# fc1 by plain tiles in every image, taps paused behind the last products of k, and the next image's sums two products later

## The chip, the cores and the metric

The kernel runs on one core of a Trainium2 chip. The metric is the device time of one execution in microseconds (us), taken as the median of several runs. The engines are TensorE (PE in the profile, with its weight loads as PEld), VectorE (DVE), ScalarE (ACT), GpSimd (POOL) and SyncE (SP). POOL and SP mostly issue DMAs here.

## What is computed

Two layers over eight images of 384 channels and 32 x 32 points, all in float32. The first is a transformer block, the second a ConvNeXt block:

```python
# layer 0, xf: (8, 1024 tokens, 384)
xn = layernorm(xf, g1, beta1)
q, k, v = split(xn @ w_qkv.T + b_qkv)              # 8 heads of 48
attn = softmax(q @ k.T * SCALE)
x1 = (attn @ v) @ w_proj.T + b_proj + xf
xn2 = layernorm(x1, g2, beta2)
y = x1 + gelu(xn2 @ w_fc1.T + b_fc1) @ w_fc2.T + b_fc2     # hidden 1536
# layer 1, on y as (8, 384, 32, 32)
z = depthwise_conv_7x7(y) + dw_b
z = layernorm_over_channels(z)
z = gelu(z @ w1 + b1)                               # hidden 1536
gx = sqrt(sum over points of z * z)
nx = gx / (mean over channels of gx + 1e-6)
z = grn_gamma * (z * nx) + grn_beta + z
out = y + z @ w2 + b2
```

## The kernel before

**Stages.** The images b = 0 to 7 follow one another. In one image PE runs the q and k products, the products of v, the attention (scores L804 and products with v L824), the projection in two halves of 512 tokens (L746), fc1 in two halves (L405), fc2 (L486), and the two products of the ConvNeXt block of the image before (h, then o). The channels are 3 tiles of 128 partitions, the hidden layer is 12 tiles, and a plain product of one hidden tile with one half is three matmuls over the channels. A float32 matmul of 512 columns shows as two records.

**Products by thirds and by quarters.** Some products use a scheme with fewer multiplications: `tiles_by_thirds` (L448) makes a group of 3 x 3 x 2 blocks out of 15 products (of sums of weights and sums of inputs) instead of 18. The 15 stand in the order SINGLY = 6, 10, 3, 5, 12, 2, 0, 11, 1, 4, 14, 7, 9, 8, 13; a callback `behind(n)` runs after product n. DVE (L473, L476) and ACT (L478) combine the results. q and k use it in images 1 to 7 (two groups: i = 0 is q, i = 1 is k). Attention starts after product 9 of k's group; the products behind it are issued at step 2 of attention (`last_tile`). fc1 uses it in images 2 to 6 (`fast_fc1`, L217) for tiles 6 to 11 of the first half, over quarters of 256 columns (`gelu_group`), with sums of weights s_fc1 that image 0 makes, and sums of inputs that ten DVE operations make (L445).

**The convolution** of image b runs beside image b + 1's attention and MLP. DVE does most taps (L1225), in a chain. ACT does HELPED of the taps per channel tile as products in half tiles (L1260), and POOL adds each to the accumulator by an accumulating DMA (L1261). The tap's tile has four buffers, so the fifth tap waits until the first has landed.

**Order.** There is no free scheduler: `Flow` (L137) adds up nominal PE time as products are issued, and issues the next piece of each DVE or ACT chain when its time has come. A chain's `yield us` sets when its next piece follows. The list `hold` pauses DVE's convolution and the chains in `freely`; the list `quiet` pauses ACT's taps. `rest()` in `mlp` (L987) runs the second half of the projection, after which LN2 of that half is spawned (`layernorm`, L527: sums L508, subtraction L551, squares L562 and L565, scaling L582).

**Layernorms.** The sums over channels are matmuls with ones. LN3 of the convolved image b − 1 runs on both halves together (`abreast`; sums L522, the subtraction L551 reads them from PSUM). LN1 of image b + 1 (`norm_of_next`, L1936) has its own sums (L1961) and subtraction L1981. Both fall in the fc1 stage of image b. PSUM has two s tiles of two banks and four o tiles of one bank; the sums and fc1's tiles share them.

**The fc1 stage of images 2 to 6**, in order: group 0 of the quarters, tiles 0 and 1, rest(), tiles 2 to 5, group 1, then twelve tiles of the second half. In images 1 and 7: tiles 0 to 3, rest(), tiles 4 to 11, then the second half.

Of the kernel before, what the change touches and what calls it, by code (L numbers as in the profile page):

```python
# [52 lines left out]
B, C, H, W = 8, 384, 32, 32  # L53
N = H * W
CT = C // P
# [9 lines left out]
CM = 2  # L65
NC = HT // CM
U = 0.857
HELPED = 6, 7, 7
BEGUN = 5
SCALE = HD ** -0.5  # L70
EPS0, EPS1, GRN_EPS = 1e-5, 1e-6, 1e-6
# [105 lines left out]
def block_kernel(  # L177
# [28 lines left out]
    flow = Flow()  # L206
# [8 lines left out]
    s_fc1 = dram.tile([P, 2, len(FORMS), P], F32, tag="s_fc1", bufs=1, name="s_fc1")  # L215

    def fast_fc1(b):  # L217
        return not exact[0] and 1 < b < B - 1

    def half(h):  # L220
        return slice(h * NH, (h + 1) * NH)
# [302 lines left out]
            totals.append((total, cols))  # L524
        return totals

    def layernorm(src, dst, h, eps, g, name, switch, spare=None, spaced=False, slow=1.0, fold=None, wait=3.4, gentle=False, late=0, lag=0, fold_squares=True):  # L527

        cols = h if isinstance(h, slice) else half(h)
        if isinstance(h, slice):
            h = h.start
        width = cols.stop - cols.start
        if spare:
            a, *squares = (t[:, :width] for t in spare())
            rstd = a
        else:
            a = one.tile([P, NH], F32, tag="ln_a", name=f"{name}_a{h}")[:, :width]  # L540
        nc.vector.tensor_tensor(a, src[:, 0, cols], src[:, 1, cols], ALU.add)
        if gentle:
            yield 1.2
        nc.vector.tensor_tensor(a, a, src[:, 2, cols], ALU.add)
        yield 2.6 * max(slow, 1.0)
        totals = yield from token_sums(a, f"{name}_sum{h}", fold, wait)
        yield 0.8
        for ct in range(CT):
            for total, part in totals:
                to, of = dst[:, ct, cols][:, part], src[:, ct, cols][:, part]  # L550
                nc.vector.scalar_tensor_tensor(to, total, -1.0 / C, of, ALU.mult, ALU.add)  # L551
            if gentle:
                yield 1.2
        yield 0.8 * slow + lag
        if not spare:
            squares = [three.tile([P, NH], F32, tag="ln_sq", name=f"{name}_sq{h}_{ct}")[:, :width] for ct in range(CT)]
        for ct in range(CT):
            nc.scalar.activation(squares[ct], dst[:, ct, cols], AF.Square)
            if spaced:
                yield 1.7  # L560
        yield 0.8 if spaced else 1.8 * slow
        nc.vector.tensor_tensor(squares[0], squares[0], squares[1], ALU.add)  # L562
        if gentle:
            yield 1.2
        nc.vector.tensor_tensor(squares[0], squares[0], squares[2], ALU.add)  # L565
        yield 1.8 * slow
        if not fold_squares:
            fold = None
            yield wait
        totals = yield from token_sums(squares[0], f"{name}_var{h}", fold, wait)  # L570
        yield 0.8

        if not spare:
            rstd = one.tile([P, NH], F32, tag="ln_rstd", name=f"{name}_rstd{h}")[:, :width]
        if switch:
            ln_table()
        for var, part in totals:
            nc.scalar.activation(rstd[:, part], var, AF.Ln, bias=eps, scale=1.0 / C)
        nc.scalar.activation(rstd, rstd, AF.Exp, scale=-0.5)
        yield (2.6 if switch else 1.2) * slow + late  # L580
        for ct in range(CT):
            nc.vector.scalar_tensor_tensor(dst[:, ct, cols], dst[:, ct, cols], col(g, ct), rstd, ALU.mult, ALU.mult)  # L582
            if gentle and ct < CT - 1:
                yield 1.2

    def averages():
        return [attn[:, i, :] for i in range(4)]
# [48 lines left out]
    def qk(b, xn, weights=None):  # L636

        big = large_tile(b)  # L640
        wqk_sb = wqk_in(big)
        parts = big[:, : 2 * NP * N].rearrange("p (i m n) -> p i m n", i=2, m=NP)
        moves = [(own, other) for i in range(2) for own, other in pieces(lambda m: parts[:, i, m, :])]

        def finish(i, m, src, cols=slice(0, N)):
            at = i * CT + m
            bias = bqk[:, at : at + 1]
            nc.scalar.activation(parts[:, i, m, cols], src, AF.Identity, bias=bias, scale=1.0 if i else SCALE)  # L648

        def move(i, m):  # L650
            for own, other in moves[2 * (i * CT + m) : 2 * (i * CT + m) + 2]:
                nc.sync.dma_start(out=own, in_=other)

        def args(i, m):
            return lambda k: wqk_sb[:, k, i * CT + m, :], lambda k: xn[:, k, :], CT

        def finishing(i, m):
            yield 1.7
            finish(i, m, parts[:, i, m, :])
            move(i, m)  # L660

        chains = {}

        def ready(m):

            for key in list(chains):
                if m in (key[1], NP - 1):
                    flow.finish(chains.pop(key))

        def plain(i, m):  # L670
            finish(i, m, linear(*args(i, m), f"qk_{b}_{i * CT + m}"))
            move(i, m)

        def fast(i):
            tiles = {}

            def bank(name):
                name = "x" if name in "jqm" else name
                if name not in tiles:
                    tiles[name] = o_tile(f"qk_{b}_{i}_{name}")  # L680
                return tiles[name]

            c = {f"c{r + 1}{n + 1}": parts[:, i, CT - 1 - r, half(n)] for r in range(CT) for n in range(2)}

            def behind(n):
                if i and n == 7:
                    hold.append("k")
                if n in (4, 9, 13):
                    m = (4, 9, 13).index(n)
                    chains[i, m] = flow.spawn(finishing(i, m))  # L690

            return tiles_by_thirds(weights, f"qk_{b}", i, thirds["qk"], c, bank, behind)

        def last_tile():

            if weights:
                flow.finish(rest_of_k)
                return
            for h in range(2):
                finish(1, CT - 1, linear_half(*args(1, CT - 1), h, f"qk_{b}_last_{h}"), half(h))  # L700
            move(1, CT - 1)

        if weights:
            for _ in fast(0):
                pass
            rest_of_k = fast(1)
            for n in rest_of_k:
                if n == 9:
                    break
            return parts[:, 0], parts[:, 1], last_tile, ready  # L710

        for m in range(CT):
            for i in range(2):
                if (m, i) != (CT - 1, 1):
                    plain(i, m)
        return parts[:, 0], parts[:, 1], last_tile, ready
# [76 lines left out]
    def attention(b, xt, qT, kT, last_tile, ready, first, next_image):  # L793
# [44 lines left out]
        for n in range(len(steps) + 2):  # L838
            if n == 1:
                hold.clear()  # L840
            if n == 2:
                last_tile()
            if n < len(steps):
                if steps[n][0] == 0 and steps[n][2] == 0:
                    ready(steps[n][1])
                ps[n] = scores(*steps[n])
            if n >= 2:
                product(*steps[n - 2], ps.pop(n - 2))
            if n - 2 in (len(steps) // 2 - 9, len(steps) - 9):
                quiet.append("averages")  # L850
            if n - 2 == len(steps) // 2 + 6:
                for chain in first:
                    flow.finish(chain)
                xn = one.tile([P, CT, N], F32, tag="xn", bufs=2, name=f"xn2_{b}")
                for m in (NP - 1, *range(CT)):
                    flow.finish(chains[0, m])
                proj(b, xt, 0)
                quiet.clear()
                next_image(b)
                slow = {1: 1.35, B - 1: 1.2}.get(b, 1.0)  # L860
                fold = "columns" if b else None
                ln = layernorm(xt, xn, 0, eps0, "g2", f"ln2_{b}", False, spaced=True, slow=slow, fold=fold, wait=4.5)
                if fast_fc1(b):
                    ln = sequence(ln, make_quarters(xn, hidden(b), 1.5))
                ln = flow.spawn(ln)
# [121 lines left out]
    def mlp(b, xt, xn, weights, tag, ln, rest, before_fc2=None, behind_ln=None):  # L987
# [9 lines left out]
        for m in range(HT // 2 if fast else HT):  # L997
# [5 lines left out]
            if m == (1 if fast else 3) and rest:  # L1003
                rest()
                slow = 0.8 if fast else 1.2 if b == 1 else 1.0
                if fast:
                    hold.append("ln2")
                ln = flow.spawn(layernorm(xt, xn, 1, eps0, "g2", f"ln2_{b}", True, slow=slow))
                behind_ln(ln)
        if fast:  # L1010
            gelu_group(hid, 1, b, weights, waiting)
# [817 lines left out]
    def main():  # L1829
# [60 lines left out]
        def conv_norm(b, ln):  # L1890
# [5 lines left out]
            else:  # L1896
# [1 line left out]
                how = dict(wait=5.0, late=3.5 if b > 1 else 0, fold_squares=b > 1) if b < B - 1 else dict(factor=2.4, slow=1.5, lag=4.0)  # L1898
                norm = abreast(acc, acc, eps1, "lnw", f"ln3_{b - 1}", True, **how)
                if b < B - 1:  # L1900
                    state["norm1"] = flow.spawn(after(ln, freely(norm_of_next(b, 22.0 if b > 1 else 28.0))))
                    state["norm3"] = flow.spawn(after(ln, freely(sequence(end_soon(b), norm))))
                else:
                    state["norm3"] = flow.spawn(after(ln, after(state["help"], after(state["conv"], norm))))
# [31 lines left out]
        def norm_of_next(b, us):  # L1936
# [62 lines left out]
            for h, a, _ in pairs:  # L1999
                for ps, view in sums[h]:  # L2000
                    nc.scalar.activation(view(a), ps, AF.Ln, bias=eps0, scale=1.0 / C)
                nc.scalar.activation(a, a, AF.Exp, scale=-0.5)
            yield 45.0
            for h, a, _ in pairs:
                for ct in range(CT):
                    part = xn[:, ct, half(h)]
# [257 lines left out]
```

## Time and profile before

| what | us |
|---|---|
| median of three runs | 3239.14 (3237.69 to 3244.53) |
| profiled execution | 3245.64 |
| its span in the profile | 3243.9 |
| granted TensorE clock, mean | 0.997 |
| fc1 stage, images 3 and 4 (first product of fc1 to first of fc2) | 76.68, 75.53 |
| same, image 6 | 76.62 |
| ACT's waits for the DMA of a tap | 24.7, 21 times |

The profile is of a single execution. PE is busy nearly throughout, so the time is in the lengths of the stages on PE: a product that waits, or that runs at a lower granted clock, makes its stage longer. In the timeline a line is a run of like instructions: start, duration, engine, line, operation, tiles, shape, count, and in brackets the idle time before and what released it. [...]

### The profile page before, as it was taken

What the parts mean: (1) busy time and instruction counts of PE and PEld (TensorE: products, weight loads), DVE (VectorE), ACT (ScalarE), POOL (GpSimd) and SP (SyncE); (2) the same over time, 40 slices, a digit from 0 to 9 for tenths busy, and PEclk for the clock granted to TensorE, in tenths of its full rate; (3) what the DMA queues carried; (4) which work ended last, traced back from release to release, by engine and by line L of the source; (5) the groups of instructions that cost most, each with busy time, mean ns of one, the idle gap of its engine ahead of it and who ended that gap; (6) DMA issues with size and microseconds to landing.
All of it is one profiled execution on the core that took longest, in us unless ns stands there. A gap on an engine that the chain in (4) does not pass through costs nothing.

```text
span 3243.9 us, 39415 instructions
## 1 busy us (share of the span) xinstructions
PE 3213.5 (99%) x14204; PEld 1402.6 (43%) x14204; DVE 2540.3 (78%) x3578; ACT 1683.6 (52%) x2389; POOL 506.5 (16%) x607
## 2 busy tenths in 40 slices
PE   9999999999999999999999999999999999999999
PEld 5344434443444434444344443444435443344454
DVE  4548788897878978688777888778887788869964
ACT  3542763447644475453753637637375374742543
POOL 2102311012120121201212012120221202200000
PEclk9999999999999999999999999999999999999999
DMA  6525832557445564546636375363843638333244
GB/s 215 191 96 190 159 71 58 156 124 159 91 88 143 140 137 90 103 131 165 130 69 132 108 186 105 76 135 103 201 96 74 140 98 204 71 78 83 65 116 113
DMA packets 208741, 396.77 MB, mean 122 GB/s; under 512 B 42912, under 2 KB 49440, under 8 KB 208160
## 3 DMA queue, kind: packets, MB, share of 16 engines
q0 software_dynamic: 81984, 167.02, 27.2%
q1 hardware_dynamic: 126272, 226.49, 23.3%
q8 instruction: 114, 1.87, 0.2%
q10 hardware_dynamic: 288, 0.71, 0.1%
q14 instruction: 83, 0.68, 0.1%
HBM read 212.98 MB, written 40.11 MB: 78 GB/s over the span
## 4 chain that ended last, share of the span: by engine, by line
PE 86%; issue 5%; DMA 4%; DVE 3%; ACT 1%; POOL 1%; SPq 0%; POOLq 0%; DVEq 0%; ACTq 0%
PE fc L405 15%; PE s L804 13%; PE o L824 12%; PE fc_p L486 11%; PE o_p L486 6%; PE v L724 4%; PE proj L746 4%; PE h_n L457 3%; DMA acc<-tap 3%; PE h_z L457 3%; PE h_x L457 3%; PE h_last L1398 2%; PE o L1349 2%; PE h L392 2%; PE h_k L457 1%
## 5 line engine op out<-in xcount | busy, mean ns | idle before, releaser
L1225 DVE SCALAR_TENSOR_TENSOR acc<-pad,vec,acc 128x930 f32<-128x930 f32 (+8 forms) x808 | 905.5, 1157 | 5.7 <-DMA acc<-tap 2.5
L813 ACT ACTIVATE p<-s 128x1024 f32<-128x1024 f32 x512 | 523.9, 1025 | 250.3 <-PE s L804 242.3
L804 PE MATMUL s<-qk 48*64 48x512 f32 x4096 | 546.7, 592 | 10.0 <-ACT qk L648 8.6
L824 PE MATMUL o<-p,v 64*64 64x512 f32 x4096 | 541.8, 588 | 0.0
L405 PE MATMUL fc<-xn,fc 128*128 128x512 f32 x972 | 430.6, 599 | 0.0
L1261 POOL DMA_DIRECT2D acc<-tap x280 | 240.6, 873 | 1164.6 <-DVE gscale L1427 504.0
L486 PE MATMUL o_p<-y,w 128*128 128x512 f32 x664 | 289.0, 593 | 0.0
L804 PEld LDWEIGHTS s<-qk 48*64 48x64 f32 x4096 | 162.7, 133 | 289.1 <-issue 210.3
L405 PEld LDWEIGHTS fc<-xn,fc 128*128 128x128 f32 x972 | 185.5, 192 | 230.9 <-issue 224.6
L824 PEld LDWEIGHTS o<-p,v 64*64 64x64 f32 x4096 | 166.7, 132 | 274.3 <-issue 266.8
L486 PE MATMUL fc_p<-qk,fc 128*128 128x512 f32 x520 | 226.9, 593 | 0.0
L1260 ACT ACTIVATE tap<-pad,vec 128x512 f32<-128x512 f32 x280 | 206.3, 738 | 24.7 <-DMA acc<-tap 24.7
L486 PEld LDWEIGHTS o_p<-y,w 128*128 128x128 f32 x664 | 125.6, 190 | 157.7 <-issue 146.4
L1225 DVE SCALAR_TENSOR_TENSOR acc_last<-pad,vec,acc_last 128x377 f32<-128x377 f32 (+24 forms) x288 | 177.2, 688 | 0.6
L486 PEld LDWEIGHTS fc_p<-qk,fc 128*128 128x128 f32 x520 | 98.4, 190 | 123.6 <-issue 119.1
L498 ACT ACTIVATE qk<-fc,bfc_f 128x512 f32<-128x512 f32 x90 | 61.1, 684 | 141.9 <-PE fc L405 141.9
L498 ACT ACTIVATE hid<-fc,bfc_f 128x512 f32<-128x512 f32 x72 | 49.3, 687 | 159.1 <-PE fc L405 159.1
L765 DVE TENSOR_TENSOR attn<-o,attn 128x512 f32<-128x512 f32 x64 | 44.1, 689 | 110.9 <-ACT attn L763 109.2
L746 PE MATMUL proj<-attn,wproj_sb 128*128 128x512 f32 x288 | 127.3, 595 | 1.1 <-ACT b_f L1706 0.6
L974 ACT COPY pad<-x 128x512 f32<-128x512 f32 x42 | 26.4, 635 | 196.1 <-DVE x L1064 196.1
L724 PE MATMUL v<-wv_sb,xn 128*128 128x384 f32 x384 | 126.8, 487 | 0.0
L724 PEld LDWEIGHTS v<-wv_sb,xn 128*128 128x128 f32 x384 | 72.5, 190 | 50.1 <-issue 3.3
(445 smaller groups left out, 4610.3 us busy)
## 6 DMA issues: line engine op xcount, KB each, us to landing
acc<-tap POOLq DMA_DIRECT2D x280, 256.0 KB, 3.7
fc<-s_fc SPq DMA_DIRECT2D x91, 256.0 KB, 4.5
w<-s_w SPq DMA_DIRECT2D x91, 256.0 KB, 2.7
w<-s_w SPq DMA_DIRECT2D x72, 320.0 KB, 4.2
fc<-in_wfc SPq DMA_DIRECT2D x54, 384.0 KB, 4.2
y<-y POOLq DMA_DIRECT2D x38, 512.0 KB, 6.8
qk<-qk POOLq DMA_DIRECT2D x30, 512.0 KB, 7.4
qk<-s_qk SPq DMA_DIRECT2D x42, 320.0 KB, 5.1
```

The costliest lines, as they stand in the source:

```text
L405: nc.tensor.matmul(out=ps, lhsT=lhsT(k), rhs=rhs(k)[:, half(h)], start=(k == 0), stop=(k == nk - 1))
L457: nc.tensor.matmul(out=at, lhsT=weights.at(wname, g, slot // 5)[:, slot % 5, :], rhs=rhs[n], start=first, stop=True, skip_group_check=not ...
L486: nc.tensor.matmul(out=bank, lhsT=lhsT, rhs=rhs, start=k == 0, stop=k == len(pairs) - 1)
L498: nc.scalar.activation(dst, src, function, **kw)
L724: nc.tensor.matmul(out=ps[:, :C], lhsT=xn[:, k, t * P : (t + 1) * P], rhs=wv_sb[:, k, :], start=(k == 0), stop=(k == CT - 1),)
L746: nc.tensor.matmul(out=ps, lhsT=wproj_sb[:, m, ct * P : (ct + 1) * P], rhs=attn[:, m, :], start=(m == 0), stop=(m == CT - 1),)
L804: nc.tensor.matmul(out=s[64 * i : 64 * i + 64, j, :], lhsT=kT[64 * j : 64 * j + HD, m, k0 : k0 + 64], rhs=qT[64 * j : 64 * j + HD, m, half ...
L813: nc.scalar.activation(p, s, AF.Exp)
L824: nc.tensor.matmul(out=outs[i][64 * j : 64 * j + 64, :], lhsT=v[keys, t, at : at + 64], rhs=p[keys, j, :], start=(t == 0), stop=(t == KT - 1),
L1225: nc.vector.scalar_tensor_tensor(dst, window, tap, dst, ALU.mult, ALU.add)
L1260: nc.scalar.mul(t.rearrange("p (h w) -> p h w", w=W), window, tap)
L1261: nc.gpsimd.dma_start(out=acc[:, ct, half(h)], in_=t, accum_op=ALU.add)
```

## The change

It has four parts.

1. `fast_fc1` is False for every image: the quarters are gone, with their DVE sums of inputs and their loads of weight sums; images 2 to 6 use the order of images 1 and 7. The pauses "group" and "ln2" go with it. The new argument `apart` of `layernorm` is never other than 0, since `fast` is False. s_fc1 is still made in image 0, and read by nothing.
2. In k's group, `quiet` gets "k" after product 2 (the sixth in order) and `hold` gets "k" after product 0 (the seventh). Before, only `hold` did, after product 7 (the twelfth). Both are cleared at step 1 of attention.
3. The delay before LN1's sums in images 2 to 6 is 25.0 for 22.0, and a later delay in the same chain is 42.0 for 45.0.
4. HELPED is 5, 7, 7 for 6, 7, 7: one tap of the first channel tile goes from ACT to DVE.

The lines of the changed kernel stand two lower from L686 on, three lower from L840 on (L746 becomes L748, L1961 becomes L1964).

```diff
-HELPED = 6, 7, 7
+HELPED = 5, 7, 7
...
     def fast_fc1(b):
-        return not exact[0] and 1 < b < B - 1
+        return False
...
-    def layernorm(src, dst, h, eps, g, name, switch, spare=None, spaced=False, slow=1.0, fold=None, wait=3.4, gentle=False, late=0, lag=0, fold_squares=True):
+    def layernorm(src, dst, h, eps, g, name, switch, spare=None, spaced=False, slow=1.0, fold=None, wait=3.4, gentle=False, late=0, lag=0, fold_squares=True, apart=0):
...
-            if gentle and ct < CT - 1:
-                yield 1.2
+            if (gentle or apart) and ct < CT - 1:
+                yield apart or 1.2
...
             def behind(n):
-                if i and n == 7:
+                if i and n == 2:
+                    quiet.append("k")
+                if i and n == 0:
                     hold.append("k")
...
             if n == 1:
                 hold.clear()
+                quiet.clear()
...
-                ln = flow.spawn(layernorm(xt, xn, 1, eps0, "g2", f"ln2_{b}", True, slow=slow))
+                ln = flow.spawn(layernorm(xt, xn, 1, eps0, "g2", f"ln2_{b}", True, slow=slow, apart=1.3 if fast else 0))
...
-                    state["norm1"] = flow.spawn(after(ln, freely(norm_of_next(b, 22.0 if b > 1 else 28.0))))
+                    state["norm1"] = flow.spawn(after(ln, freely(norm_of_next(b, 25.0 if b > 1 else 28.0))))
...
-            yield 45.0
+            yield 42.0
```

## The prediction

> **What bounds the kernel now.** I read four views in this order: the head of the page, the chain of waits, the table of windows over the fc1 stages, and the waits of PE with the timeline around the two longest.
>
> ```profile
> span 3243.9 us, 39415 instructions
> ...
> PE 3213.5 (99%) x14204; PEld 1402.6 (43%) x14204; DVE 2540.3 (78%) x3578; ACT 1683.6 (52%) x2389; POOL 506.5 (16%) x607
> ...
> PE 86%; issue 5%; DMA 4%; DVE 3%; ACT 1%; POOL 1%; SPq 0%; POOLq 0%; DVEq 0%; ACTq 0%
> ```
>
> PE sets the end. It never rests for long, so time can only be won by fewer products, or by products that run at full pace. At full pace a product (two records of 512 columns) takes 0.858 us (records follow each other every 0.429 us in the timeline). "Busy 99%" hides slow products: a matmul that waits or runs at a lower clock counts as busy. So I compare lengths of like stages, from the fc1 stage's first product to fc2's first (the columns are busy time of PE, weight loads, DVE, ACT and POOL, then the clock, the DMA share and GB/s):
>
> ```profile
> 479.31:552.84 73.53, 73.53 (x184) 31.91 (x183) 60.03 (x77) 27.10 (x38) 8.97 (x10) 1.00 0.23 46
> 873.50:950.12 76.62, 74.66 (x208) 37.04 (x207) 53.67 (x88) 33.37 (x54) 9.76 (x11) 0.98 0.32 70
> ...
> 2065.11:2140.47 75.36, 73.27 (x210) 36.37 (x207) 52.78 (x86) 32.58 (x52) 9.32 (x11) 1.00 0.32 71
> ```
>
> The first row is image 1, which already runs fc1 by plain tiles: 73.53 us. Images 2 to 6 run the quarters: 76.62, 76.68, 75.53, 75.36, 76.62, together 380.81. The form with fewer multiplications is the longer one. Where it goes:
>
> ```profile
> PE s L804 <- ACT qk L648: 8.6, 7, 2.4
> PE fc_n L457 <- DVE qk L473: 8.0, 5, 1.6
> PE ln_sum L1961 <- PE ln_sum L1961: 1.7, 5, 0.4
> ...
> ACT tap L1260 <- DMA acc<-tap: 24.7, 21, 3.2
> ```
>
> The second line is the quarters' own wait, 1.6 us in each of five images. The first is the start of attention behind the k tiles; the last is ACT held by a tap's buffer. The third looks like nothing, yet what follows it in image 3 is dear:
>
> ```profile
> 1337.60 1.08 PE L522 MATMUL ln_sum<-attn,ones 64*64 64x512 f32 x4
> 1338.61 0.71 PE L1961 MATMUL ln_sum<-ln,ones 32*128 32x256 f32 x6
> 1339.65 0.67 PE L1961 MATMUL ln_sum<-ln,ones 32*128 32x256 f32 x2 [0.34 <-PE ln_sum L1961]
> 1340.25 8.83 PE L405 MATMUL fc<-xn,fc 128*128 128x512 f32 x16
> ```
>
> Its windows:
>
> ```profile
> 1336.50:1340.20 3.70, 3.36 (x17) 1.02 (x16) 2.53 (x5) 0.00 (x0) 0.00 (x0) 1.00 0.19 63
> 1340.20:1344.20 4.00, 4.00 (x7) 1.65 (x7) 4.00 (x9) 1.70 (x3) 0.00 (x0) 0.57 0.00 0
> ```
>
> 3.7 us of partial-array sums, then 4.0 us at a granted clock of 0.57: sixteen records took 8.83 us, where 16 × 0.429 = 6.9.
>
> **What the Trainium skill says.** "TensorE: Matmul & The Clock Gate", Part 1 (The HAM clock gate): the clock is half or full, decided by activity over windows of about 3.4 us. The trace agrees (0.57 over the 4.0 us after the sums; 1.00 in images 4 and 5 at the same place, so whether a window is caught depends on phase). The same page, "Architectural detail", says ACT and DVE run strictly in order. The trace agrees: L648 stands behind a tap that waits up to 3.2 us for a DMA. "Trainium Kernel Development and Optimization", Key Constraints: all queues' DMAs share the same 16 engines. The trace agrees where taps land late: the DMA share is 0.85 at the k boundary of image 7.
>
> **The change part by part.**
>
> *1. Quarters to plain tiles, five images.* A quarter group's start-to-next-start is 6.83 us (7.16 in image 5) for group 0 and 8.45 for group 1 with its 1.6 us wait, 15.3 together; 18 plain products are 18 × 0.858 = 15.44. Cost: +0.16 × 5 = +0.8 us, the lost multiplications paid by the lost wait. Ten DVE operations per image (L445, 413 ns) and three chunk loads on SP's queue go too; neither was on PE's path. With the loads gone the residual rows of the projection (r, L785) are no longer queued behind weights on SP.
>
> *2. Projection and LN2.* rest() moves from after tile 1 to after tile 3: the second projection half starts 12 products, about 10.3 us, into the stage instead of 12.0–12.3, and needs its last operand about 1.7 us later, at 12.0. That operand (L791, 685 ns) ended 11.1–13.4 us in, in images 2–6, at 10.14 in image 1. I bound the wait by 0 (image 1) and 1.4 us (13.4 − 12.0), and take 0.3 per image, 1.5 in all, because the loads that delayed r are gone. LN2 loses its hold, so DVE's taps (1.157 us) stand between its operations. Image 1 runs so already: its last L582 ended at 516.6, the second half began about 519.6, 3 us to spare.
>
> *3. Sums.* The next image's first sums (L1961, then L1964) now stand two products behind LN3's (L522), then one product follows. The eight-bank PSUM is what still binds: fc1's next bank waits for three L551 (3 × 0.611), the sums' bank for the other three. From the order in which instructions stand, two products (1.7 us) plus the sums (1.0) reach the bank 0.3–0.4 us too early, twice. Estimated loss 1.5 us per image with L522's own cost, 7.5 in all. Before, L522, L1961 and the slow products cost 4.30, 4.34, 3.09, 2.67, 4.30 = 18.7 over their full-pace time, image 1 0.94. Gain 18.7 − 7.5 = 11.2. The yield of 42 for 45 keeps the end of norm_of_next where it was.
>
> Parts 1–3 check against the stage lengths: 380.8 − 5 × 73.53 = 13.2 if the five stages were as short as image 1's; less 5 × 0.55 for the sums left together, less 1.5 for the projection: 8.9. The terms give 11.2 − 0.8 − 1.5 = 8.9.
>
> *4. The k boundary.* Before, only the convolution was held, from the twelfth of 15 products; now ACT's taps pause from the sixth and DVE's from the seventh, until the second step of attention. 28 products are 24.02 us; the seven q/k stages (images 1–7) took 24.13, 24.74, 26.60, 25.45, 25.50, 25.07, 26.63: 9.96 over. In image 3 the cause is plain:
>
> ```profile
> 1147.85 0.74 ACT L1260 ACTIVATE tap<-pad,vec 128x512 f32<-128x512 f32 x1 [2.53 <-DMA acc<-tap]
> 1148.49 1.13 ACT L648 ACTIVATE qk<-qk,bqk 128x1024 f32<-128x1024 f32 x1
> ```
>
> PE at the same place, and in image 7, with a window of image 7:
>
> ```profile
> 1149.68 1.95 PE L804 MATMUL s<-qk 48*64 48x512 f32 x16 [1.96 <-ACT qk L648]
> ...
> 2736.84 3.69 PE L804 MATMUL s<-qk 48*64 48x512 f32 x16 [2.43 <-ACT qk L648]
> ...
> 2733.00:2745.00 12.00, 9.57 (x36) 2.83 (x38) 6.95 (x10) 7.41 (x8) 4.22 (x5) 0.72 0.85 176
> ```
>
> Image 7 also restarts slowly: sixteen scores in 3.69 us instead of 1.95, and its attention is 124.54 us where others have 122.1–122.5. With no tap ahead of the last L648, I leave 0.15 per image: gain 9.0, plus about 2.0 in image 7's attention: 11.
>
> Queued behind the pause: some ten ACT taps with their POOL accumulations, and DVE's chain. Neither is due until LN3, in the fc1 stage. There the burst of ten taps that ended the convolution at about 38.6 us falls away; in the new order the last DVE tap stands at 35.2 and the last ACT tap at 24.0.
>
> *5. HELPED 6 to 5.* One tap per image from ACT to DVE, 7 × 1.157 = 8.1 us on an engine 78% busy; hidden beside PE, cost 0; if the convolution's end came to bind, up to 8.1.
>
> *6. fc2.* LN3's six L582 (742 ns) now stand before the differences that fc2 needs. In the new order these (L1067) come about 0.7 us ahead of need; range 0 to 0.7 × 5 = 3.5 us lost. I take 0, since the 8.9 above already carries a cautious projection.
>
> **Sum.** 8.9 + 11 = 20 us. The profiled execution took 3245.64 (span 3243.9 and 1.7 around it) and would become 3225.7. The median is 6.5 us lower, so I carry the same saving over: 3239.1 − 20 = 3219.
>
> **The rivals.**
>
> *A, forecast (0.60):* both stalls go, residuals as above. 3219, own range 3213 to 3226.
>
> *B, half of it (0.15):* the stall moves. The bank waits still trip the clock in three images (about 1.7 us more each, 5.1), the differences for fc2 come 0.7 late in five (3.5), k keeps a third of its loss (3.3): gain 8, 3231. For it: one tap still stands ahead of the last L648.
>
> *C, more (0.10):* no clock dips and no residuals: 13.2 + 12.5 with the other attentions' slight losses (images 3, 4 and 6, 0.5 us each): about 3213.
>
> *D, a trade (0.08):* the slow window comes wherever sums stand, so step 3's 11.2 are gone, and the paused taps crowd into the first steps of attention and give back 7 of the 11 at k: 20 − 11.2 − 7 leaves 2, so 3237. Against: image 1 shows sums that stand apart, without a dip.
>
> *E, slower (0.07):* LN2 without its hold. Six dependent DVE steps each wait behind one tap of 1.157 us, 6.9 us, plus the projection's 1.4; less image 1's 3 us of slack, 5.3 us of idle PE before the second half, in five images, and an idle of that length brings a slow-clock window, about 1.7 us more: 7.0 × 5 = 35. Then 3239 − 20 + 35 = 3254. It decides from 4 us per image on (20 / 5). For it: DVE's instructions in the new order, times their durations, make about 32 us of work for the 35 us concerned. Against: image 1.
>
> **How the numbers follow.** The measurement can tell about 0.2%, 6.5 us. A, most of B and C are faster by more: 0.84. D with B's tail is within: 0.09. E: 0.07. Range 3210 to 3235: it holds A and C nearly whole and B; left out are E and most of D.
>
> **What would show it.** fc1 stages of images 2–6 near 74.5 us; no L457 wait on L473; L1964 no longer beside L522, clock 1.00 in the eight us behind L522; no L1260 between the last k product and L648, the wait of scores on L648 under 2 us in sum; q/k stages at 24.1–24.3. Against me: a wait of the projection on L793 over 1 us, a wait on xn (L582) at the second half, a wait of fc2 on L1067, or a granted clock under 0.9 behind L522.

## The result, and the profile after

The changed kernel took 3224.26 us (median of six runs, 3223.74 to 3229.43); the kernel before, run again beside it, 3244.51 (3237.69 to 3249.71). The ratio is 0.9945, 95% interval 0.993 to 0.9959: faster by 13 to 23 us. The profiled execution went from a span of 3243.9 us to 3222.6, 21.3 us less. The prediction was 20 us less, and 3219.

The head of the page and the waits of PE, after:

```profile
span 3222.6 us, 38795 instructions
...
PE 3207.6 (100%) x14084; PEld 1376.6 (43%) x14084; DVE 2490.1 (77%) x3425; ACT 1662.6 (52%) x2325; POOL 494.7 (15%) x593
...
PE 93%; issue 2%; DMA 2%; DVE 1%; POOL 1%; ACT 0%; SPq 0%; POOLq 0%; DVEq 0%; ACTq 0%
```

```profile
PE h_n L457 <- DVE y L473: 2.9, 6, 0.5
...
PE h_k L457 <- DVE y L476: 1.0, 5, 0.2
...
PE s L806 <- ACT qk L648: 0.2, 1, 0.2
PE proj L748 <- DVE attn L793: 0.2, 1, 0.2
```

The scores' wait on L648 went from 8.6 us to 0.2, and the quarters' wait on L473 is gone. On top stands a wait that was not there before: the h products (the first product of the ConvNeXt block) wait for DVE's combinations.

PE is busy in both kernels, so the account is again one of stage lengths, from one stage's first product on PE to the next one's. The sums are over the images named. Of the rest, image 0's attention is 0.3 us shorter, image 7 from fc1 to the end of the kernel 0.4 longer, and the other stages changed by 0.1 us or less.

| stage (us) | before | after | gain | predicted |
|---|---|---|---|---|
| q/k, images 1 to 7 | 178.12 | 168.91 | 9.2 | 9.0 |
| attention, images 1 to 7 | 858.03 | 851.57 | 6.5 | 2.0 |
| fc1 with the second projection half, images 2 to 6 | 380.80 | 369.55 | 11.3 | 8.9 |
| fc2, images 1 to 6 | 321.86 | 321.86 | 0.0 | 0 |
| h, images 1 to 6 | 312.99 | 318.24 | −5.3 | 0 |

Two of the windows over fc1, after (the first is image 1, the second image 3), with the columns as before:

```profile
479.10:552.76 73.66, 73.66 (x184) 31.92 (x183) 63.44 (x80) 27.26 (x38) 8.87 (x10) 1.00 0.23 46
...
1265.84:1339.72 73.88, 73.76 (x186) 32.04 (x183) 49.22 (x71) 33.46 (x48) 13.25 (x16) 1.00 0.30 57
```

And the k boundary of image 3 after, ACT and then PE:

```profile
1141.24 0.59 ACT L478 COPY qk<-qk_x 128x512 f32<-128x512 f32 x1 [0.27 <-PE qk_x L457]
1142.89 1.15 ACT L648 ACTIVATE qk<-qk,bqk 128x1024 f32<-128x1024 f32 x1 [1.07 <-DVE qk L473]
```

```profile
1143.61 1.02 PE L457 MATMUL qk_n<-thirds,qk 128*128 128x512 f32 x2
1144.56 1.95 PE L806 MATMUL s<-qk 48*64 48x512 f32 x16
```

No tap stands between the copy and L648 now. L648 waits for its operand only, and the scores follow k's last product without an idle bracket.

### The profile page after: what moved, and what is told of

Its sections match the earlier page's. It is cut to its first block, busy times and chain, and to the rows that moved or that the text cites. A ratio compares the mean times of both kernels' runs of the same rounds, so it can differ in the third digit from the quotient of the medians.

```text
span 3222.6 us, 38795 instructions
## 1 busy us (share of the span) xinstructions
PE 3207.6 (100%) x14084; PEld 1376.6 (43%) x14084; DVE 2490.1 (77%) x3425; ACT 1662.6 (52%) x2325; POOL 494.7 (15%) x593
## 4 chain that ended last, share of the span: by engine, by line
PE 93%; issue 2%; DMA 2%; DVE 1%; POOL 1%; ACT 0%; SPq 0%; POOLq 0%; DVEq 0%; ACTq 0%
PE fc L405 17%; PE s L806 12%; PE o L826 12%; PE fc_p L486 11%; PE o_p L486 11%; PE proj L748 4%; PE v L726 3%; PE h_n L457 3%; PE h_z L457 2%; PE h_x L457 2%; PE h_last L1401 2%; PE o L1352 2%; PE h L392 2%; PE qk_n L457 2%; PE qk_z L457 2%
## 5 line engine op out<-in xcount | busy, mean ns | idle before, releaser
L1228 DVE SCALAR_TENSOR_TENSOR acc<-pad,vec,acc 128x870 f32<-128x870 f32 (+8 forms) x815 | 909.5, 1157 | 2.5
L806 PE MATMUL s<-qk 48*64 48x512 f32 x4096 | 539.3, 590 | 0.2 <-ACT qk L648 0.2
L405 PE MATMUL fc<-xn,fc 128*128 128x512 f32 x1152 | 505.5, 594 | 0.6
L1264 POOL DMA_DIRECT2D acc<-tap x266 | 227.4, 861 | 1357.6 <-ACT tap L1263 642.9
L405 PEld LDWEIGHTS fc<-xn,fc 128*128 128x128 f32 x1152 | 216.6, 190 | 280.6 <-issue 261.4
L486 PE MATMUL fc_p<-hid,fc 128*128 128x512 f32 x728 | 319.0, 594 | 0.0
L498 ACT ACTIVATE hid<-fc,bfc_f 128x512 f32<-128x512 f32 x192 | 131.6, 686 | 343.7 <-PE fc L405 343.6
L486 PEld LDWEIGHTS fc_p<-hid,fc 128*128 128x128 f32 x728 | 137.4, 190 | 174.9 <-issue 169.3
L1263 ACT ACTIVATE tap<-pad,vec 128x512 f32<-128x512 f32 x266 | 195.1, 736 | 5.3 <-DMA acc<-tap 5.3
L748 PE MATMUL proj<-attn,wproj_sb 128*128 128x512 f32 x288 | 127.4, 596 | 0.8 <-ACT b_f L1709 0.6
L551 DVE SCALAR_TENSOR_TENSOR acc<-ln_sum,acc 128x512 f32<-128x512 f32 x42 | 25.7, 681 | 93.6 <-PE ln_sum L522 93.6
```

The source lines that it names most:

```text
L405: nc.tensor.matmul(out=ps, lhsT=lhsT(k), rhs=rhs(k)[:, half(h)], start=(k == 0), stop=(k == nk - 1))
L486: nc.tensor.matmul(out=bank, lhsT=lhsT, rhs=rhs, start=k == 0, stop=k == len(pairs) - 1)
L498: nc.scalar.activation(dst, src, function, **kw)
L748: nc.tensor.matmul(out=ps, lhsT=wproj_sb[:, m, ct * P : (ct + 1) * P], rhs=attn[:, m, :], start=(m == 0), stop=(m == CT - 1),)
L806: nc.tensor.matmul(out=s[64 * i : 64 * i + 64, j, :], lhsT=kT[64 * j : 64 * j + HD, m, k0 : k0 + 64], rhs=qT[64 * j : 64 * j + HD, m, half ...
L1228: nc.vector.scalar_tensor_tensor(dst, window, tap, dst, ALU.mult, ALU.add)
```

## The experiments

Every time is compared with runs of the kernel before on the same chip, so the ratios can be set side by side; the changed kernel's is 0.9945. The four below ran first.

**k_only: the pause alone.**

```diff
 # in the kernel before
-                if i and n == 7:
+                if i and n == 2:
+                    quiet.append("k")
+                if i and n == 0:
                     hold.append("k")
...
             if n == 1:
                 hold.clear()
+                quiet.clear()
```

> The kernel before with the pause of the taps behind k alone (ACT's taps from the sixth of k's products, DVE's from the seventh, both until step 1 of attention). Theory: the last bias addition of k (L648) no longer stands behind a tap that waits for a DMA; the seven q/k stages take 24.1 us each (9 us in sum), and the attentions of images 2 to 7 lose their slow starts (5 to 6 us): 14 to 15 us faster than before, about 3229; the fc1 stages stay at 75.4 to 76.7. Rival (the paused taps crowd into attention and fc1 and take it back): the q/k stages shorten, but attention or fc1 grow, and no more than 7 us are left.

3230.55 us, ratio 0.9965 (0.9953 to 0.9977), 11 us faster. In its profile all seven q/k stages are 24.13 us, and the attentions of images 1 to 7 add up to 851.69, as after. These two give 15.5 us, of which 11.1 are left in the span, because this execution's attention of image 0 took 137.26 us instead of 133.41 (last section). The fc1 stages stayed long. The theory holds for the stages; the median is 3 us short of the lower end of what I expected, though 14 us lies within the interval. A pause moves taps, and nothing of the q/k gain came back elsewhere.

**no_k: the changed kernel without the pause.**

```diff
 # in the changed kernel
-                if i and n == 2:
-                    quiet.append("k")
-                if i and n == 0:
+                if i and n == 7:
                     hold.append("k")
...
-                quiet.clear()
```

> The changed kernel with the old pause behind k (the convolution alone, from the twelfth product). Theory: the q/k stages are back at 24.7 to 26.6 us and attention at 122.5: 14 to 15 us slower than the changed kernel, about 3239. Rival (plain fc1 and the tap moved from ACT had a share in it): less than 8 us slower.

3241.06 us, ratio 0.9993 (0.9984 to 1.0001): about 15.6 us above the changed kernel by the ratios. q/k stages 24.13 to 26.03. Without the pause, the other three parts together can hardly be told from no change. In its profile they do show: the fc1 stages are 10.9 us shorter in sum, the h stages 5.3 longer. The gains of k_only and no_k add up to 13.6 us where the changed kernel has 17.8 by its ratio; the intervals are wide enough for that.

**plain_only: plain fc1 alone** (the quarters' two pauses go with it).

```diff
 # in the kernel before
     def fast_fc1(b):
-        return not exact[0] and 1 < b < B - 1
+        return False
```

> The kernel before with fc1 by plain tiles in all images, and nothing else. Theory (the sums that stand together are what made the fc1 stage long, not the quarters): LN1's sums still follow LN3's at once, so the fc1 stages of images 2 to 6 stay at about 76 us, within 1 us of before, and the h stages grow by 1 us each because LN1's scaling comes earlier: 2 to 6 us slower than before. Rival (the quarters' wait on DVE and their loads were the cost): fc1 stages of about 74 us, 6 to 11 us faster than before.

3240.36 us, ratio 1.0 (0.9991 to 1.0008). Neither came true as a whole. The fc1 stages fell to 74.75 to 74.79, 373.8 in sum: 7.0 us less than before. The h stages of images 2 to 6 grew by 0.68 each, 3.4 in sum. The sums in image 3, and windows from them on:

```profile
1327.63 0.65 PE L522 MATMUL ln_sum<-ln_a,ones 64*64 64x512 f32 x2
1327.64 0.65 PE L522 MATMUL ln_sum<-attn,ones 64*64 64x512 f32 x2
1328.11 0.60 PE L522 MATMUL ln_sum<-ln_a,ones 64*64 64x512 f32 x2
1328.12 0.59 PE L522 MATMUL ln_sum<-attn,ones 64*64 64x512 f32 x2
1328.65 0.71 PE L1961 MATMUL ln_sum<-ln,ones 32*128 32x256 f32 x8
1330.78 4.53 PE L405 MATMUL fc<-xn,fc 128*128 128x512 f32 x10 [1.42 <-DVE acc L551]
```

```profile
1327.60:1330.80 3.20, 1.78 (x18) 0.57 (x17) 2.05 (x4) 0.69 (x1) 0.69 (x1) 1.00 0.68 118
1330.80:1334.80 4.00, 4.00 (x10) 1.85 (x11) 4.00 (x8) 1.72 (x4) 0.00 (x0) 1.00 0.27 45
```

Two things differ from before. LN3's two groups of sums start together (1327.63 and 1327.64) where they ran one after the other (1336.54 and 1337.60), and the clock behind them is full. The bank wait is not gone, it is 1.42 us in one piece. A slow window behind the sums cost 1.55, 1.81 and 1.62 us in images 2, 3 and 6 before, 5.0 of the 7.0.

**old_sums: the changed kernel with the old delays.**

```diff
 # in the changed kernel
-norm_of_next(b, 25.0 if b > 1 else 28.0)
+norm_of_next(b, 22.0 if b > 1 else 28.0)
...
-            yield 42.0
+            yield 45.0
```

> The changed kernel with the old delays of LN1's chain (22 and 45), so that LN1's sums follow LN3's at once. Theory: the fc1 stages of images 2 to 6 are back at about 76 us, with a granted clock below 0.9 behind the sums in some of them: 9 to 12 us slower than the changed kernel, about 3234. Rival (the plain order alone mends it): within 2 us of the changed kernel, fc1 stages at 74 us.

3229.98 us, ratio 0.9964 (0.995 to 0.9978), about 6 us above the changed kernel; its profile has one of the long attentions of image 0 (137.28). The fc1 stages are 74.70 each, 4.0 in sum over the changed kernel's, with the same wait of 1.4 us for L551 behind L1964 as in plain_only and no slow window. So most of what I had put down to the two products' distance comes with the plain order already.

The next four went together.

**late_scale: where LN1's scaling falls.**

```diff
 # in the changed kernel
-            yield 42.0
+            yield 51.0
```

> The changed kernel with one number altered: the later delay in LN1's chain is 51 where it is 42, so that LN1's scaling (L2010) stands 13.8 us into the h stage instead of 5.2 (before: 12.0). Theory (the h stages of images 2 to 6 grew from 52.17 to 53.15 us because DVE does LN1's scalings there just where a group's first results must be combined): the h stages are back at 52.2, about 5 us faster than the changed kernel, near 3219. Rival (the tap that went from ACT to DVE did it): the h stages stay at 53.15 and the time stays.

3224.38 us, ratio 0.9944 (0.9933 to 0.9956). The h stages are 52.95, not 52.2: neither side. In the trace the first scaling starts 14.7 us into the stage, and PE's wait for L473 has moved on by one product, from h_n to h_z (2.6 us in six waits).

**helped6: the moved tap put back.**

```diff
 # in the changed kernel
-HELPED = 5, 7, 7
+HELPED = 6, 7, 7
```

> The changed kernel with HELPED back at 6, 7, 7. Theory (the moved tap lies beside PE's work wherever it is): within 2 us of the changed kernel, the h stages still 53.15. Rival (the tap on DVE crowds the h stage): the h stages go to 52.2 and the kernel is 5 us faster.

3225.82 us, ratio 0.9945 (0.9933 to 0.9957), h stages 53.15. The tap is hidden in either place, and is not what lengthens the h stages.

**act_pause and dve_pause: one engine's taps paused, not both.**

```diff
 # act_pause, in the changed kernel
-                if i and n == 0:
+                if i and n == 7:
                     hold.append("k")
 # dve_pause, in the changed kernel
-                if i and n == 2:
-                    quiet.append("k")
```

> The changed kernel with ACT's taps paused from the sixth of k's products as it has it, but DVE's convolution held only from the twelfth, as before. Theory (an ACT tap that waits for its buffer ahead of L648 was the whole cause): q/k stages of 24.1 us, within 2 us of the changed kernel. Rival (DVE's taps delay the combination that L648 reads): q/k stages of 24.5 to 25, 3 to 6 us slower than the changed kernel.

> The changed kernel with DVE's convolution held from the seventh of k's products as it has it, but no pause of ACT's taps. Theory: q/k stages of 24.7 to 26.6 us, 12 to 16 us slower than the changed kernel, as with the old pause. Rival: q/k stages near 24.5, less than 6 us slower.

act_pause: 3226.1 us, ratio 0.9946 (0.9934 to 0.9957), q/k stages 24.13 in all images. dve_pause: 3238.76, ratio 0.9987 (0.998 to 0.9993), q/k stages up to 26.64. ACT's pause is the whole of the k gain, as far as the intervals tell. ACT at the boundary of image 3 in dve_pause:

```profile
1146.05 0.59 ACT L478 COPY qk<-qk_x 128x512 f32<-128x512 f32 x1
1148.02 0.74 ACT L1261 ACTIVATE tap<-pad,vec 128x512 f32<-128x512 f32 x1 [1.38 <-DMA acc<-tap]
1148.66 1.13 ACT L648 ACTIVATE qk<-qk,bqk 128x1024 f32<-128x1024 f32 x1
```

The tap is back ahead of L648, with its DMA wait, though DVE's chain was held. That the wait counts, and not the tap, is seen in the kernel before: in images 2 to 7 the tap ahead of the last L648 had waited 1.5 to 3.2 us, and the stages are 0.6 to 2.5 us longer than 24.13; in image 1 two taps stand there that waited for nothing, and the stage is 24.13.

**scale49, sums28_45, sums18_56: the h stages and the sums again.** By the nominal PE time that orders the instructions, all three put LN1's scaling 12.0 us into the h stage, where the kernel before had it, and the changed kernel 5.2; in the trace its first operation then starts 14.1 us into the stage before and in scale49, and 5.4 after. The last two move the sums as well.

```diff
 # scale49, in the changed kernel
-            yield 42.0
+            yield 49.0
 # sums28_45: 28.0 and 45.0 for 25.0 and 42.0
 # sums18_56: 18.0 and 56.0 for 25.0 and 42.0
```

> The changed kernel with the later delay of LN1's chain at 49, where it is 42: LN1's scaling stands 12.0 us into the h stage, just where the kernel before had it (51 put it at 13.8, 42 at 5.2). Theory (what counts is where in a group of h products DVE's scaling falls, and before it fell where no combination was due): the h stages of images 2 to 6 are back at 52.2 us, about 5 us off the profiled span, near 3219 in the median. Rival (something else of the plain order sits in the h stage): 52.9 or more, as with 51.

3221.8 us, ratio 0.9935 (0.9919 to 0.9951); the span is 2.7 us shorter. The h stages of images 2 to 6 are 52.18, 52.18, 52.17, 52.17 and 52.43; that of image 1 grew from 52.51 to 53.61, since the same number moves its scaling too. Together 3.5 us less. In the h stage of image 3 of the changed kernel PE waits twice, 0.21 and 0.55 us. DVE's first scaling there, and what stands on DVE and PE at the second wait:

```profile
1398.64 0.74 DVE L2010 SCALAR_TENSOR_TENSOR xn<-xn,vec,ln 128x512 f32<-128x512 f32 x1
...
1410.30 1.09 DVE L1244 SCALAR_TENSOR_TENSOR begun<-pad,vec,begun 128x841 f32<-128x841 f32 x1
1411.30 0.75 DVE L2010 SCALAR_TENSOR_TENSOR xn<-xn,vec,ln 128x512 f32<-128x512 f32 x1
1411.97 0.68 DVE L473 TENSOR_TENSOR y<-h_n,y 128x512 f32<-128x512 f32 x1
```

```profile
1412.70 1.12 PE L457 MATMUL h_n<-acc,w 128*128 128x512 f32 x2 [0.55 <-DVE y L473]
```

And the first scaling before, then in scale49, and there the same product, which does not wait:

```profile
1416.60 0.74 DVE L2007 SCALAR_TENSOR_TENSOR xn<-xn,vec,ln 128x512 f32<-128x512 f32 x1
```

```profile
1408.55 0.75 DVE L2010 SCALAR_TENSOR_TENSOR xn<-xn,vec,ln 128x512 f32<-128x512 f32 x1
```

```profile
1412.82 1.13 PE L457 MATMUL h_n<-acc,w 128*128 128x512 f32 x2
```

The h stage starts at 1393.28 after, at 1402.47 before and at 1394.43 in scale49. Six scalings of 0.74 us do not fill DVE. But a tap and a scaling stand ahead of the combination that frees the bank of the next h_n product, and which combinations the scalings stand ahead of makes 1 us per image. In the profiles of the other runs, too, the stage's length goes with the place of the first scaling: at 7.0 us into the stage (plain_only, old_sums) it takes 52.85 us, at 13.5 (quarters_free, below) 52.63, at 14.7 (late_scale) 52.95.

> The changed kernel with the delays of LN1's chain at 28 and 45 (25 and 42): LN1's sums follow LN3's after four products instead of two, and LN1's scaling stands 12.0 us into the h stage. Theory (the bank of LN1's sums and that of fc1's next tile then come free before they are wanted): the fc1 stages fall from 73.89 to 73.1 to 73.3 us and the h stages to 52.2: 8 us faster than the changed kernel, near 3216. Rival (later sums push LN1's subtractions against LN3's scaling, and fc2 waits for its differences): fc2 stages grow above 53.6 and the gain is 5 us or less.

3225.49 us, ratio 0.9941 (0.9924 to 0.9957). The fc1 stages fell to 73.40 (73.61 in image 6), as the theory has it, and the h stages are short; but fc2 grew from 53.56 to 54.40 in five images, 4.2 us. The stages did what the rival said, with this wait on top of PE's list:

```profile
PE fc_p L486 <- DVE x L1064: 3.9, 5, 0.8
```

Its way was another, though: L1064 does not make fc2's differences, it adds the bias to a result of fc2 and frees its bank, and in image 3 it stands behind LN3's six scalings (L582) on DVE.

> The changed kernel with the delays at 18 and 56: LN1's sums come 4 us before LN3's, as they do in image 1, and LN1's scaling stands 12.0 us into the h stage. Theory (sums that stand apart cost about 0.94 us a stage, as in image 1, against 1.57): fc1 stages of about 73.3, h stages of 52.2: 8 us faster than the changed kernel. Rival (LN1's fold DMAs have not landed so early): PE waits for a DMA at L1964 and the fc1 stages grow above 74.

3217.59 us, ratio 0.9921 (0.9905 to 0.9937): the fastest of all, about 8 us below the changed kernel by the ratios, 6 by the spans. The fc1 stages are 73.49, the fc2 stages 53.57, the h stages 52.17 to 52.60. PE does not wait for a DMA at L1964:

```profile
1319.06 0.71 PE L1964 MATMUL ln_sum<-ln,ones 32*128 32x256 f32 x8
1319.71 3.70 PE L405 MATMUL fc<-xn,fc 128*128 128x512 f32 x8
1323.34 0.65 PE L522 MATMUL ln_sum<-ln_a,ones 64*64 64x512 f32 x2
```

**quarters_free: the quarters without their pauses.** The last run asked why plain fc1 alone gained 7 us. In the trace of before, the fold of LN3's second half was issued at 1331.28 with 6.2 us to landing, and the second group of sums started at 1337.60, which looks like a wait for that fold. (A fold is a DMA that adds one half of the partitions to the other.)

```diff
 # in the kernel before
             if fast and m == 0:
-                hold.append("group")
                 gelu_group(hid, 0, b, weights)
...
-                if fast:
-                    hold.append("ln2")
...
-norm_of_next(b, 22.0 if b > 1 else 28.0)
+norm_of_next(b, 24.0 if b > 1 else 28.0)
...
-            yield 45.0
+            yield 49.0
```

> The kernel before, quarters and all, without the two pauses that went with them (hold "group" and "ln2"), and with the delays of LN1's chain at 24 and 49, so that LN1's sums still follow LN3's at once. The convolution then ends about 5 us earlier in the fc1 stage, and LN3's folds start earlier. Theory (plain fc1 gained 7 us over five images because LN3's second sums no longer waited for a fold's DMA that started late, not because the quarters went): the two groups of L522 run together, no slow clock follows, and the fc1 stages of images 2 to 6 fall from 76.2 to about 74.8, as with plain fc1 alone. Rival (the quarters themselves are dear): the stages stay above 75.8.

3277.99 us, ratio 1.0111 (1.0094 to 1.0128): 33 us slower. The fc1 stages took 80.0 to 83.6 us, because DVE's taps now stand in the quarters' own chain:

```profile
PE fc_n L457 <- DVE qk L473: 12.2, 10, 1.6
PE fc_z L457 <- DVE qk L473: 10.4, 6, 2.0
```

As to the sums the run does not test the theory, for the wait that it was to remove is still there. The two groups of L522 ran one after the other again, and in images 2 and 5 a slow window of 1.8 and 1.6 us followed. In image 3 DVE had LN3's operands ready at 1331.31, but POOL issues the folds, and there they stand behind the DMA of fc_e, which waits for ACT. POOL, the time from issue to landing (the last column), and PE:

```profile
1340.45 1.22 POOL L970 DMA_DIRECT2D fc_e<-qk  x1 [13.30 <-ACT fc_e L969]
1341.21 1.37 POOL L516 DMA_DIRECT2D ln_a<-ln_a  x1
1341.74 1.67 POOL L516 DMA_DIRECT2D attn<-attn  x1
```

```profile
ln_a<-ln_a POOLq DMA_DIRECT2D x1, 128.0 KB, 5.6
attn<-attn POOLq DMA_DIRECT2D x1, 128.0 KB, 6.1
```

```profile
1347.00 1.08 PE L522 MATMUL ln_sum<-ln_a,ones 64*64 64x512 f32 x4
1347.98 1.08 PE L522 MATMUL ln_sum<-attn,ones 64*64 64x512 f32 x4
```

1341.74 and 6.1 make 1347.84: the second group starts as its fold lands. The traces of before and k_only say the same: in all 15 stages of images 2 to 6 with quarters it starts 0.1 us behind the landing. In the 55 stages with plain fc1 that the eleven other profiles hold, the second fold had landed 8 us or more before, and the groups start within 0.1 us of each other. Why the folds are late in the kernel before is seen on DVE in image 3, where ten taps in a row stand ahead of LN3's operands; the fold of the second half before, and then after with its time to landing:

```profile
1315.59 11.56 DVE L1225 SCALAR_TENSOR_TENSOR acc<-pad,vec,acc 128x841 f32<-128x841 f32 x10
```

```profile
1331.28 1.62 POOL L516 DMA_DIRECT2D attn<-attn  x1
```

```profile
1308.48 2.19 POOL L516 DMA_DIRECT2D attn<-attn  x1
```

```profile
attn<-attn POOLq DMA_DIRECT2D x1, 128.0 KB, 4.2
```

That is 59.0 us into the stage before, and 42.6 after. The rival's number came true, but not through the quarters' own price, which the trace of before gives (next section). What this run shows is what the two pauses bought.

## Why the prediction was right, and where it was not

- **The k boundary** (predicted 11, of which 9.0 in the q/k stages and 2.0 in attention): 9.2 and 6.5. The mechanism is shown by act_pause and dve_pause. The term that was too small is attention: I counted image 7's slow restart only (it gave 3.0), but images 2 to 6 gave 3.4 more. k_only has the same, so the pause gives it; at which of attention's waits was not followed. Rival C had 1.5 of that.
- **The sums** (11.2). From the first sum to fc2's first product, less 0.429 us for each record of fc1 in between, the five stages lose 24.0 us before and 12.3 after: 11.8 less. (The prediction's 18.7 leaves out the sums' own time, and takes in 0.5 us of image 4 from ahead of them.) The size was right, and its attribution was not. The step gave all of it to the delays 25 and 42. In plain_only the same count is 16.4, so 4.1 are the delays', as old_sums also shows, and 7.7 come with the plain order: 5.0 for the slow windows, and 2.7 are left for the second group's wait. The step had missed that wait for a fold, although the prediction names what causes it: the burst of ten taps that falls away, to which it gives no gain. The wait is read from the traces, in every stage; no run moved the folds alone. The slow window came in 8 of the 15 stages with the wait and in none of the 55 without; why in some of the 15 and not in others is open.
- **Quarters for plain tiles** (−0.8): what is left of the five fc1 stages without that loss, the projection included, is 356.8 us before and 357.3 after. The 0.5 us is less than the 2.3 that this term and the next have together. The lost wait pays for the multiplications nearly in full.
- **Projection and LN2** (−1.5): PE's wait on L793 is 0.2 us in the whole profile, in image 0, and no stage of images 2 to 6 is more than 0.1 longer than the others. It was right that image 1's order carries over; the caution was not needed. Two readings were off: r (L785) holds no residual, but the reciprocals of the softmax sums, and in images 2 to 6 before its product (L791) ended 11.9 to 13.2 us in, not 11.1 to 13.4.
- **The h stages** (not in the sum): −5.3. This is the step that failed. I wrote that the yield of 42 for 45 keeps the end of norm_of_next where it was. It does not: the pauses that went with the quarters had delayed this chain too. LN1's scaling started 14.1 us into the h stage of image 3 before (1416.60 against 1402.47), 7.0 in plain_only, which keeps the old delays, and 5.4 after (1398.64 against 1393.28). helped6 clears the tap, scale49 brings four of five stages back to 52.2, so the place of the scaling is the cause.
- **fc2 and HELPED** (0 and 0): fc2 is 53.56 us in both, and helped6 is the same as the changed kernel.

So that 20 came so close to 21.3 was luck in part, two errors that offset each other: attention and fc1 gave about 7 more than the sum had, the h stages took 5.3. The 5 us between 3219 and 3224 are the kernel before: 3239 in the three runs shown, 3244.5 in the six.

The rivals: B's wait of fc2 for its differences (L1067) is in no profile; sums28_45, with the sums two products further on, has one for L1064. E needed LN2 to be late; no wait for it is in the profile. D's half (k taps crowding attention) is refuted by k_only.

## What to carry to other kernels

An engine that works in order and does spare work for another needs that spare work out of the way ahead of its own urgent instruction: here one ACT tap of 0.74 us per image, with a wait of up to 3.2 us for a buffer, cost 15 us in the stages of seven images (11 in the median of k_only), and pausing DVE's larger work made no difference that could be measured. POOL was such an engine too, where the folds stood behind another transfer (quarters_free). When a pause is taken out, look at every chain that it paused: LN1's scaling, of no concern to the quarters, moved by 9 us and cost a fifth of what the rest gained. "It stays where it was" is a claim to be checked in the new order of instructions, like any other.

## What was not expected of the hardware

- The attention of image 0 is the same code in all fourteen profiled kernels, and took 133.1 to 133.9 us in eight of the profiles and 137.3 to 139.0 in six. In k_only the 4 us lie at the first projection half: from its first product to the next scores it took 12.5 us there, and 8.4 in the changed kernel's profile. PE waited for L793, which waits for the DMA of its reciprocals (it starts at 141.64 in k_only and at 138.88 after), and the clock then fell. k_only:

```profile
142.38 7.97 PE L748 MATMUL proj<-attn,wproj_sb 128*128 128x512 f32 x14 [2.63 <-DVE attn L793]
```

The window from 142.2 on, with the clock as its third number from the end:

```profile
142.20:146.20 4.00, 3.82 (x6) 1.69 (x7) 0.88 (x2) 0.00 (x0) 0.00 (x0) 0.69 0.95 336
```

- Sums that use part of the array were followed by a slow clock or not according to how they pack, as far as these runs go: with L522's groups apart, in 8 of 15 stages, even though PE hardly idled (3.36 us busy of 3.70 in image 3 before); with the groups together, never, even with 1.42 us of idle behind them (plain_only, old_sums).
